# Normalising tokens from PSUM on VectorE instead of from SBUF on GpSimd, in a convolution-attention and mixture kernel on one Trainium2 core

## Chip, core and metric

The kernel runs on one core of one Trainium2 chip. A core has TensorE (matrix products, in the profile PE for the products and PEld for loading the stationary operand), VectorE (DVE), ScalarE (ACT), GpSimd (POOL) and SyncE (SP), which here only issues transfers. The engines run side by side, each takes its own instructions strictly in order, and they wait for each other through semaphores. SBUF is the working memory, PSUM the smaller memory into which TensorE writes. The metric is the device time of one execution in microseconds (us); a profile of one execution is the other source. All data is 32-bit floating point.

## What is computed

Eight images of 128 channels and 36 x 36 = 1296 positions pass through two layers. Cut to what matters here:

```python
# layer 0: group norm, then a convolution-attention block, added to x
q = conv3x3(x1); k = conv3x3(x1); v = conv3x3(x1)         # keys and values on 34 x 34 positions
a = einsum('ncd,nqd->ncq', v, softmax(einsum('ncd,ncq->nqd', k, q)))
x = x + conv1x1(tanh(conv1x1(concat([x1, a]))))
# layer 1: additive attention over the 1296 tokens of each image
t = tokens(x); y = layernorm(t)                           # over the 128 channels
s[i, j] = sum_d w[d] * tanh(q[i, d] + k[j, d]) + bw       # q, k: linear maps of y
t = t + softmax(s, axis=-1) @ y
# 64 experts, each picks 8 tokens of every image
z = layernorm(t)
gate = softmax(z @ gate_w.T, axis=tokens); top 8 per expert; gather; two layers; scatter-add
```

The tanh of every pair of tokens is the bulk of the work. The kernel writes it through products of exponentials: for each pair of token blocks it forms numerators n and denominators d by matrix products of features `qf` and `kf`, and needs n/d summed over the feature groups.

## The kernel before

**The main loop.** The pairwise stage is cut into units (image b, chunk c of 432 query tokens, tile j of 128 key tokens): 8 x 3 x 11 = 264 units. Ten of the eleven tiles have 12 slots each, the last tile (16 remaining tokens) has 3, so there are 2952 slots, in one static order. Each slot p issues, in this order: `take_turns(p)` (what background steps have to do outside TensorE); `numerators(p)`, two products into two PSUM buffers `n` (L793, or L800 for the short tile); `denominators(p + 3)`, two products into `d` and the logarithm of both by ScalarE (L815), and on every second slot one exponential over two slots' worth (L818), which makes 1/d; `terms(p)`, in which VectorE multiplies n by 1/d; and `matmul_turn(p)`, which lets background work put matrix products behind the slot's own. In 8 of 12 slots VectorE writes two products `rp` (L846) and GpSimd adds them to a running sum `accp` (L851 for the first, L853 after); in the other 4 VectorE multiplies in PSUM and adds to its own sum `accd` (L835 to L842). At the end of a unit GpSimd folds both sums (L860, L863) and ScalarE exponentiates (L878). `rp` has three buffers, so VectorE may run about two slots ahead of GpSimd and no more.

**Background work.** Everything else is written as generators in four lanes: `first_of_all` (query features), `urgent` (`attend`), `gates` (`gating`) and `background` (`normal`, `conv_keys`, `layer0`, `tokens` and `keys` of the next image). A generator yields either `step(rest)` (run my next part in take_turns, after `rest` slots) or `matmuls(rest)` (my next part issues matrix products), and `TAKE` after products, so that their reader runs one slot later. Products are counted in columns plus 20 each (`bmm` L237, `turned_to` L241 for transposes); a slot earns 370 of them, and while the balance is negative only `first_of_all` gets a turn. The order of the instructions on every engine comes out of this when the program is built; nothing is decided on the chip. For the first image all this runs ahead of the main loop, one generator after the other (`drain`).

**PSUM.** The pool `ps_n` has four buffers. The two `n` of every slot and the buffer of every background group (`aux`) come out of it in turn, so a background buffer that is read late holds up a later slot's products.

**The four places that the change touches.**

- `layer0`, per chunk of 432 positions: scores `s0`, exponentials `ex` on ScalarE (L381), their total on GpSimd (`total`, L374), ten products with the values in five pairs, each pair summed in a PSUM buffer `pa0` and added to `ax` in SBUF by VectorE (L395 the first, L397 the others, with a factor 1/D). Then the total over partitions by a product with ones (`pt0`), its reciprocal `ri` by two ScalarE instructions (L405, L406), a product `px1`, and VectorE's `ax * ri` (L412) and sum into `hp` (L413).
- `tokens`: the image is transposed into token rows, three PSUM buffers of four, four and three tiles (`tpl`), copied to `tok` in SBUF (L510, L516), sent to DRAM, and its mean and variance taken (L525, L526). After the reciprocal root on GpSimd (`rsqrt`, L218), GpSimd normalises the 11 tiles from `tok` into `xh` (L538), two at a time, one slot between. `xh` is transposed back into `xT` (`tpc`, L556).
- `attend`, four times per chunk: 11 products over the exponentials in two groups of six and five (`pa1`). VectorE copies the first group to `sums` (L625), adds the second (L628), takes the reciprocal of the last column (L630), and adds the scaled row to the token in `t2` (L631), then takes mean and variance (L635, L636).
- `gate_logits`: `t2` is transposed (`tp2`, L241), copied to `tt` (L676) and sent to DRAM; GpSimd normalises the 12 tiles of `t2` in place (L681), two at a time; then they are transposed again into `xc` (L691) and multiplied by the gating weights (L696). For the last image this runs per chunk, behind each `attend`.

**After the loop** come the last chunk's attending and gating, the experts with 32 MB of weights, and the scatter by matrix products.

Of the kernel before, what the change touches and what calls it, by code (L numbers as in the profile page):

```python
# [17 lines left out]
D = HV * WV  # L18
# [46 lines left out]
def kernel(  # L65
# [55 lines left out]
    with ExitStack() as loop, ExitStack() as score:  # L121
# [25 lines left out]
        def chunk_tile(name):  # L147
            return chunks.tile([128, CH], F32, tag="chunk", name=name)

        def aux(name):  # L150
            return ps_n.tile([128, 512], F32, tag="n", name=name)
# [177 lines left out]
        def layer0(b):  # L329

            r = xs[b][:, :N]
            k = convolved.pop("k")
            while gates:
                yield step()
            wv_t = load_taps(w_v, "wv_t")
            v = big_tile("v0")
            wq_t = load_taps(w_q, "wq_t")
            yield matmuls(3)
            for r0, nr in KROWS:
                yield from conv_turns(  # L340
                    wv_t, (r0, nr), 1, 1, WV, v[:, r0 * WV : (r0 + nr) * WV]
                )
            yield matmuls(1)

            vw = big_tile("vw")[:DT, : NDT * C].rearrange("p (j c) -> p j c", c=C)
            for g in range(0, NDT, 4):
                some = DTILES[g : g + 4]
                tp = aux("pvw")
                for j, (o, n) in enumerate(some):
                    bmm(tp[:n, j * C : (j + 1) * C], v[:, o : o + n], wh_s[:, 1, :],  # L350
                       start=True, stop=True)
                yield TAKE
                full = sum(n == DT for _, n in some)
                nc.vector.tensor_copy(
                    vw[:, g : g + full, :],
                    tp[:DT, : full * C].rearrange("p (j c) -> p j c", c=C),
                )
                for j in range(full, len(some)):
                    n = some[j][1]
                    nc.vector.tensor_copy(vw[:n, g + j, :], tp[:n, j * C : (j + 1) * C])  # L360
                yield matmuls()
            hp = big_tile("hpre")[:, :N]
            for c in range(NCH):
                cols = slice(c * CH, (c + 1) * CH)
                q = chunk_tile("q0")
                yield from conv_turns(wq_t, (c * RC, RC), 0, 0, W, q)
                yield matmuls(1)
                tot = chunk_tile("tot0")
                ex = []

                def total(j):
                    n = DTILES[j][1]
                    of = ex[0] if j == 1 else tot
                    nc.gpsimd.tensor_add(tot[:n], of[:n], ex[j][:n])  # L374

                for o, n in DTILES:
                    ps = aux("s0")
                    bmm(ps[:n, :CH], k[:, o : o + n], q, start=True, stop=True)
                    yield TAKE
                    e = chunk_tile("e0")  # L380
                    nc.scalar.activation(e[:n], ps[:n, :CH], AF.Exp)  # L381
                    ex.append(e)
                    if len(ex) > 2:
                        total(len(ex) - 2)
                    yield matmuls()
                ax = chunk_tile("ax0")
                for j0 in range(0, NDT, 2):
                    pa = aux("pa0")
                    for j in (j0, j0 + 1):
                        n = DTILES[j][1]  # L390
                        bmm(pa[:, :CH], vw[:n, j, :], ex[j][:n], start=(j == j0), stop=(j > j0))
                    yield TAKE
                    if j0 == 0:
                        total(NDT - 1)
                        nc.vector.tensor_scalar(ax, pa[:, :CH], 1.0 / D, None, ALU.mult)  # L395
                    else:
                        nc.vector.scalar_tensor_tensor(  # L397
                            ax, pa[:, :CH], 1.0 / D, ax, ALU.mult, ALU.add
                        )
                    yield matmuls()  # L400
                pt = aux("pt0")
                bmm(pt[:, :CH], ones[:DT], tot[:DT], start=True, stop=True)
                yield TAKE
                ri = chunk_tile("ri0")
                nc.scalar.activation(ri, pt[:, :CH], AF.Ln, scale=1.0 / D)  # L405
                nc.scalar.activation(ri, ri, AF.Exp, scale=-1.0)  # L406
                yield matmuls(1)
                px = aux("px1")
                bmm(px[:, :CH].rearrange("p (a b) -> p a b", b=W), wh_s[:, 0, :],
                   xpad[:, 1 + c * RC : 1 + (c + 1) * RC, 1 : 1 + W], start=True, stop=True)  # L410
                yield TAKE
                nc.vector.tensor_mul(ax, ax, ri)  # L412
                nc.vector.tensor_add(hp[:, cols], px[:, :CH], ax)  # L413
                yield matmuls()
            yield step(2)
            nc.scalar.activation(hp, hp, AF.Tanh, bias=hb)
            nc.scalar.preload_act_table_set(LNEXP)
            yield matmuls(2)
            for c in range(NCH):
                cols = slice(c * CH, (c + 1) * CH)  # L420
                po = aux("po0")
                bmm(po[:, :CH], wo_s, hp[:, cols], start=True, stop=True)
                yield TAKE
                nc.vector.scalar_tensor_tensor(
                    r[:, cols], po[:, :CH], bo_s, r[:, cols], ALU.add, ALU.add
                )
                yield matmuls()
# [63 lines left out]
        def tokens(b):  # L491
# [40 lines left out]
            rsqrt(rs, ve)  # L532
            xh = big_tile("xh")[:, : NKT * (C + 1)].rearrange("p (t c) -> p t c", c=C + 1)
            nc.gpsimd.memset(xh[:, :, C : C + 1], 1.0)
            yield step()
            for t in range(NKT):
                n = KT[t][1]
                nc.gpsimd.tensor_scalar(  # L538
                    xh[:n, t, :C], tok[:n, t, :], mv[:n, t, 0:1], rs[:n, t : t + 1],
                    ALU.subtract, ALU.mult,  # L540
                )
                if t % 2 == 1:
                    yield step()
            xT = big_tile("xT")[:, :N]
            yield matmuls(2)
            for g in range(0, NKT, 4):
# [54 lines left out]
        def attend(b, c, es):  # L601
# [8 lines left out]
            for i in range(TPC):  # L610
                at = c * TPC + i
                nc.sync.dma_start(t2[:T, at, :], tokd[b][at * T : (at + 1) * T])
                sums = two.tile([T, C + 1], F32, tag="sums", name="sums")
                for some in (range(6), range(6, NKT)):
                    pa = aux("pa1")[:T, : C + 1]
                    for j in some:
                        if j < NKT - 1:
                            e, v = es[j][:, i * T : (i + 1) * T], xh[:, j, :]
                        else:
                            rows = slice(32 * i, 32 * i + REM)  # L620
                            e, v = es[j][rows, :T], xr[rows]
                        bmm(pa, e, v, start=(j == some[0]), stop=(j == some[-1]))
                    yield TAKE
                    if j < NKT - 1:
                        nc.vector.tensor_copy(sums, pa)  # L625
                        yield matmuls()
                    else:
                        nc.vector.tensor_add(sums, pa, sums)  # L628
                inv = small.tile([T, 1], F32, tag="inv", name="inv")
                nc.vector.reciprocal(inv, sums[:, C : C + 1])  # L630
                nc.vector.scalar_tensor_tensor(  # L631
                    t2[:T, at, :], sums[:, :C], inv, t2[:T, at, :], ALU.mult, ALU.add
                )
                st = small.tile([T, 6], F32, tag="t2_st", name="t2_st")
                nc.vector.bn_stats(st, t2[:T, at, :])  # L635
                nc.vector.bn_aggr(mv[:, at, :], st)  # L636
                yield matmuls()
# [11 lines left out]
        def gate_logits(b, chunks):  # L649
# [23 lines left out]
            for c in chunks:  # L673
                tp, tt = turned(c, "t2T")
                yield TAKE
                nc.vector.tensor_copy(tt, tp[:, :CH])  # L676
                nc.sync.dma_start(t2d[b][:, c * CH : (c + 1) * CH], tt)
                yield matmuls()
            yield step()
            for j, t in enumerate(tiles):  # L680
                nc.gpsimd.tensor_scalar(  # L681
                    t2[:T, t, :], t2[:T, t, :], mv[:, t, 0:1], rs[:, j : j + 1],
                    ALU.subtract, ALU.mult,
                )
                if t % 2 == 1:
                    yield step()
            yield matmuls(2)
            for c in chunks:
                tp, xc = turned(c, "xc")
                yield TAKE  # L690
# [458 lines left out]
```

## Time and profile before

| | |
|---|---|
| median of three runs | 6428.76 us (6428.02 to 6435.07) |
| the profiled execution | 6428.41 us |
| its span, first to last instruction | 6426.7 us |
| PE busy | 6054.8 us (94%) |
| ACT busy | 5354.6 us (83%) |
| DVE busy | 4900.4 us (76%) |
| POOL busy | 4798.1 us (75%) |
| mean granted TensorE clock | 0.966 |

Busy time is the union of an engine's instructions; matrix products are pipelined, so a busy PE is not PE at its peak. Beside busy time the profile has groups of instructions (line, engine, names of what is written and read, shapes, count, busy time, mean duration of one in ns, idle time of the engine before them and what ended it), the waits (which engine's instruction was released by whose, in all), the chain (the work that ended last, followed back from the last instruction) and a timeline. A line of a group can be that of a helper: all background products stand under L237 and all background transposes under L241, told apart by the names of their tiles.

### The profile page before, as it was taken

The numbers are of one execution on the slowest core, as the hardware profiler recorded it, in microseconds if no ns is written. First come the engines' busy times: TensorE is split into PE (matmuls) and PEld (weight loads), VectorE is DVE, ScalarE is ACT, GpSimd is POOL, SyncE is SP. The second block draws the span as 40 slices with busy tenths as digits, with TensorE's granted clock in tenths as the row PEclk, the third lists the DMA queues.
The fourth block names the chain that finished last, engine by engine and source line by source line (L and its number), as shares of the span: only waits on it lengthen the run. The fifth ranks groups of instructions, "written<-read, shape, count | busy, mean of one in ns | idle before, by whom it ended". The sixth has DMA issues, their size and how long they took to land.

```text
span 6426.7 us, 106771 instructions
## 1 busy us (share of the span) xinstructions
PE 6054.8 (94%) x40448; PEld 2813.9 (44%) x40448; DVE 4900.4 (76%) x9315; ACT 5354.6 (83%) x5426; POOL 4798.1 (75%) x2966
## 2 busy tenths in 40 slices
PE   8999999999999999999999999999999999999986
PEld 4444444444444444444444444444444444544432
DVE  3687778877788777888788887887778877778862
ACT  1788898888888888888888888888888888989970
POOL 3677777787777877777787787778777787888870
PEclk9999999999999999999999999999999999999997
DMA  0200011000110002100111001100011000100017
GB/s 28 66 31 23 22 63 36 30 24 27 56 46 19 24 27 68 33 26 22 44 47 38 22 23 53 43 32 25 20 63 43 23 24 27 61 26 28 24 66 253
DMA packets 155284, 265.78 MB, mean 41 GB/s; under 512 B 53712, under 2 KB 79824, under 8 KB 154768
## 3 DMA queue, kind: packets, MB, share of 16 engines
q1 hardware_dynamic: 154768, 258.95, 12.5%
q8 instruction: 318, 5.21, 0.3%
q14 instruction: 198, 1.62, 0.1%
HBM read 196.81 MB, written 61.83 MB: 40 GB/s over the span
## 4 chain that ended last, share of the span: by engine, by line
PE 67%; DVE 12%; ACT 7%; issue 7%; POOL 6%; DMA 1%; SPq 0%; POOLq 0%; DVEq 0%; ACTq 0%
PE n L793 30%; PE d L793 10%; PE pc L237 7%; PE pa L237 6%; ACT lq L815 5%; DVE n L840 3%; DVE rp L846 3%; PE s L237 3%; PE pk L237 3%; PE pq L237 2%; DVE accd L842 2%; POOL accp L853 2%; DVE t L631 1%; PE n L800 1%; POOL t L681 1%
## 5 line engine op out<-in xcount | busy, mean ns | idle before, releaser
L853 POOL TENSOR_TENSOR accp<-accp,rp 128x864 f32<-128x864 f32 x1464 | 2965.2, 2025 | 1028.0 <-DVE rp L846 975.3
L793 PE MATMUL n<-qf,kf 32*128 32x432 f32 (+1 forms) x11520 | 3239.2, 579 | 93.4 <-DVE rp L846 47.0
L815 ACT ACTIVATE lq<-d 128x864 f32<-128x864 f32 x2952 | 2552.6, 882 | 690.7 <-PE d L793 643.3
L793 PE MATMUL d<-qf,kf 32*128 32x432 f32 (+1 forms) x11520 | 2876.6, 568 | 21.2 <-ACT lq L815 16.4
L846 DVE TENSOR_TENSOR rp<-n,lq 128x432 f32<-128x432 f32 x3984 | 2202.6, 600 | 623.7 <-PE d L793 399.3
L818 ACT ACTIVATE lq<-lq 128x1728 f32<-128x1728 f32 x1488 | 2429.0, 1632 | 47.1
L793 PEld LDWEIGHTS n<-qf,kf 32*128 32x128 f32 (+1 forms) x11520 | 1167.1, 187 | 1703.4 <-DVE rp L846 586.3
L793 PEld LDWEIGHTS d<-qf,kf 32*128 32x128 f32 (+1 forms) x11520 | 1038.8, 188 | 392.2 <-issue 254.1
L840 DVE TENSOR_TENSOR n<-n,lq 128x432 f32<-128x432 f32 x1440 | 811.7, 608 | 280.1 <-PE n L793 239.2
L842 DVE TENSOR_TENSOR accd<-n,accd 128x432 f32<-128x432 f32 x1440 | 867.4, 602 | 24.7
L851 POOL TENSOR_TENSOR accp<-rp 128x864 f32<-128x864 f32 x264 | 533.8, 2022 | 221.1 <-DVE rp L846 217.5
L237 PE MATMUL pa<-xh,e 128*108 128x129 f32 x1920 | 262.6, 284 | 55.6 <-DVE rp L846 34.7
L860 POOL TENSOR_TENSOR accp<-accp 128x432 f32<-128x432 f32 x264 | 290.8, 1101 | 16.2
L237 PEld LDWEIGHTS pa<-xh,e 128*108 128x108 f32 x1920 | 223.3, 175 | 179.1 <-DVE rp L846 107.4
L594 POOL TENSOR_SCALAR qf<-qf,cs_s 128x432 f32<-128x432 f32 x192 | 262.7, 1374 | 42.0 <-ACT qf L593 42.0
L863 POOL TENSOR_TENSOR accd<-accp,accd 128x432 f32<-128x432 f32 x240 | 265.6, 1107 | 28.5 <-DVE accd L842 10.4
L237 PE MATMUL s<-q,k 128*116 128x432 f32 x480 | 229.8, 570 | 3.3 <-DVE q L260 2.1
L237 PEld LDWEIGHTS pk<-xT,a_k 128*128 128x128 f32 x1408 | 172.2, 193 | 109.8 <-DVE accd L842 27.6
L374 POOL TENSOR_TENSOR tot<-tot,e 116x432 f32<-116x432 f32 x192 | 212.0, 1104 | 6.1
L835 DVE TENSOR_TENSOR accd<-n,lq 128x432 f32<-128x432 f32 x240 | 144.9, 604 | 91.6 <-PE n L793 60.5
L381 ACT ACTIVATE e<-s 116x432 f32<-116x432 f32 x240 | 125.0, 521 | 106.6 <-PE s L237 105.5
L237 PE MATMUL pk<-xT,a_k 128*128 128x128 f32 (+1 forms) x1408 | 203.2, 288 | 2.6 <-DVE accd L842 2.3
(175 smaller groups left out, 4144.4 us busy)
## 6 DMA issues: line engine op xcount, KB each, us to landing
kf<-kd SPq DMA_DIRECT2D x240, 512.0 KB
kd<-ks SPq DMA_DIRECT2D x160, 256.0 KB
w<-in_weight_dram SPq DMA_DIRECT2D x32, 1024.0 KB
x<-in_x_dram SPq DMA_DIRECT2D x8, 648.0 KB
t<-tokd SPq DMA_DIRECT2D x96, 54.0 KB
t2d<-t2T SPq DMA_DIRECT2D x24, 216.0 KB
res<-t2d SPq DMA_DIRECT2D x8, 648.0 KB
out_dram<-res SPq DMA_DIRECT2D x8, 648.0 KB
```

The costliest lines, as they stand in the source:

```text
L237: mm(out, lhsT, rhs, **kw)
L594: nc.gpsimd.tensor_scalar(qf[:, 1, :], qf[:, 0, :], cs_s[:, q : q + 1], None, ALU.mult)
L793: mm(outs[h][:, :CH], kf[rows[h], q, :], qf_of[b, c, q][rows[h], part, :], start=True, stop=True)
L815: nc.scalar.activation(lq[:, o : o + 2, :], d[:, :, :CH], AF.Ln)
L818: nc.scalar.activation(some, some, AF.Exp, scale=-1.0)
L840: mult(ns[h], ns[h], lq[:, o + h, :])
L842: nc.vector.tensor_add(live["d"], ns[h], live["d"])
L846: mult(rp[:, h, :], ns[h], lq[:, o + h, :])
L851: nc.gpsimd.tensor_add(live["p"], live["r"], rp)
L853: nc.gpsimd.tensor_add(live["p"], live["p"], rp)
L860: nc.gpsimd.tensor_add(s[:, 0, :], s[:, 0, :], s[:, 1, :])
L863: nc.gpsimd.tensor_add(d, s[:, 0, :], d)
```

## The change

In `tokens` and in `gate_logits` the normalisation is no longer made by GpSimd from SBUF. TensorE transposes the image (or the transposed tokens `tt`) once more into PSUM, and VectorE normalises from there into SBUF. In `attend` the second group's sum, its reciprocal and the scaled addition read PSUM. In `layer0` the total over partitions and its reciprocal come before the last pair of products, the factor 1/D is dropped (it cancelled), and the last partial sum is added in PSUM and multiplied by `ri` from there.

```diff
 layer0
                 ax = chunk_tile("ax0")
+                ri = chunk_tile("ri0")
                 for j0 in range(0, NDT, 2):
-                    pa = aux("pa0")
+                    if j0 == NDT - 2:
+                        pt = aux("pt0")
+                        bmm(pt[:, :CH], ones[:DT], tot[:DT], start=True, stop=True)
+                        yield TAKE
+                        nc.scalar.activation(ri, pt[:, :CH], AF.Ln)
+                        nc.scalar.activation(ri, ri, AF.Exp, scale=-1.0)
+                        yield matmuls()
+                    pa = aux("pa0")[:, :CH]
...
                     if j0 == 0:
                         total(NDT - 1)
-                        nc.vector.tensor_scalar(ax, pa[:, :CH], 1.0 / D, None, ALU.mult)
+                        nc.vector.tensor_copy(ax, pa)
+                    elif j0 < NDT - 2:
+                        nc.vector.tensor_add(ax, pa, ax)
                     else:
-                        nc.vector.scalar_tensor_tensor(
-                            ax, pa[:, :CH], 1.0 / D, ax, ALU.mult, ALU.add
-                        )
+                        nc.vector.tensor_add(pa, pa, ax)
+                        nc.vector.tensor_mul(ax, pa, ri)
                     yield matmuls()
-                pt = aux("pt0")
-                bmm(pt[:, :CH], ones[:DT], tot[:DT], start=True, stop=True)
-                yield TAKE
-                ri = chunk_tile("ri0")
-                nc.scalar.activation(ri, pt[:, :CH], AF.Ln, scale=1.0 / D)
-                nc.scalar.activation(ri, ri, AF.Exp, scale=-1.0)
-                yield matmuls(1)
                 px = aux("px1")
...
                 yield TAKE
-                nc.vector.tensor_mul(ax, ax, ri)
                 nc.vector.tensor_add(hp[:, cols], px[:, :CH], ax)
 tokens
-            yield step()
-            for t in range(NKT):
-                n = KT[t][1]
-                nc.gpsimd.tensor_scalar(
-                    xh[:n, t, :C], tok[:n, t, :], mv[:n, t, 0:1], rs[:n, t : t + 1],
-                    ALU.subtract, ALU.mult,
-                )
-                if t % 2 == 1:
-                    yield step()
+            yield matmuls()
+            for g in range(0, NKT, 4):
+                tp = aux("tpn")
+                some = list(range(g, min(g + 4, NKT)))
+                for t in some:
+                    o, n = KT[t]
+                    turned_to(tp[:n, (t - g) * C : (t - g + 1) * C], r[:, o : o + n], ident)
+                yield TAKE
+                for t in some:
+                    n = KT[t][1]
+                    nc.vector.tensor_scalar(
+                        xh[:n, t, :C], tp[:n, (t - g) * C : (t - g + 1) * C],
+                        mv[:n, t, 0:1], rs[:n, t : t + 1], ALU.subtract, ALU.mult,
+                    )
+                yield matmuls()
 attend
-                    else:
-                        nc.vector.tensor_add(sums, pa, sums)
+                nc.vector.tensor_add(pa, pa, sums)
                 inv = small.tile([T, 1], F32, tag="inv", name="inv")
-                nc.vector.reciprocal(inv, sums[:, C : C + 1])
+                nc.vector.reciprocal(inv, pa[:, C : C + 1])
                 nc.vector.scalar_tensor_tensor(
-                    t2[:T, at, :], sums[:, :C], inv, t2[:T, at, :], ALU.mult, ALU.add
+                    t2[:T, at, :], pa[:, :C], inv, t2[:T, at, :], ALU.mult, ALU.add
                 )
 gate_logits
-                yield matmuls()
-            yield step()
-            for j, t in enumerate(tiles):
-                nc.gpsimd.tensor_scalar(
-                    t2[:T, t, :], t2[:T, t, :], mv[:, t, 0:1], rs[:, j : j + 1],
-                    ALU.subtract, ALU.mult,
-                )
-                if t % 2 == 1:
-                    yield step()
-            yield matmuls(2)
+                yield matmuls(1)
+                tp = aux("tp3")
+                for j in range(TPC):
+                    turned_to(tp[:T, j * C : (j + 1) * C], tt[:, j * T : (j + 1) * T], ident)
+                yield TAKE
+                for j in range(TPC):
+                    t = c * TPC + j
+                    nc.vector.tensor_scalar(
+                        t2[:T, t, :], tp[:T, j * C : (j + 1) * C],
+                        mv[:, t, 0:1], rs[:, t - tiles[0] : t - tiles[0] + 1],
+                        ALU.subtract, ALU.mult,
+                    )
+                yield matmuls(1)
             for c in chunks:
                 tp, xc = turned(c, "xc")
```

More of the change, by code (lines that the diff above doesn't have):

```diff
@@ L386, in layer0 @@
                 ax = chunk_tile("ax0")
+                ri = chunk_tile("ri0")
                 for j0 in range(0, NDT, 2):
-                    pa = aux("pa0")
+                    if j0 == NDT - 2:
[6 more added lines that the diff above has]
+                    pa = aux("pa0")[:, :CH]
                     for j in (j0, j0 + 1):
                         n = DTILES[j][1]
-                        bmm(pa[:, :CH], vw[:n, j, :], ex[j][:n], start=(j == j0), stop=(j > j0))
+                        bmm(pa, vw[:n, j, :], ex[j][:n], start=(j == j0), stop=(j > j0))
                     yield TAKE
```

## The prediction

> **What bounds the kernel now.** I read the busy times first, then the chain, the waits, the groups by shape, the windows around the two normalisations, and the timeline inside them. From the page:
>
> ```profile
> PE 6054.8 (94%) x40448; PEld 2813.9 (44%) x40448; DVE 4900.4 (76%) x9315; ACT 5354.6 (83%) x5426; POOL 4798.1 (75%) x2966
> PE 67%; DVE 12%; ACT 7%; issue 7%; POOL 6%; DMA 1%; SPq 0%; POOLq 0%; DVEq 0%; ACTq 0%
> ```
>
> The second line is the chain: TensorE sets the pace in most places, GpSimd 6% and VectorE 12% of the span. Summed by name, the chain's pieces hold POOL t L681 57.5 us, POOL xh L538 32.2 and DVE t L631 83.8. These three are what the change attacks. The waits of VectorE on GpSimd, and who waits for L538:
>
> ```profile
> DVE rp L846 <- POOL accp L851: 78.1, 32, 8.7
> PEld tpc L241 <- POOL xh L538: 21.8, 17, 9.0
> ```
>
> The groups by shape (count | busy us, mean ns):
>
> ```profile
> L631 DVE SCALAR_TENSOR_TENSOR t<-sums,inv,t 108x128 f32<-108x128 f32 x96 | 87.9, 915 | 29.0 <-DMA t<-tokd 25.7
> L681 POOL TENSOR_SCALAR t<-t,t_mv,t_rs 108x128 f32<-108x128 f32 x96 | 75.0, 792 | 0.1
> L538 POOL TENSOR_SCALAR xh<-tok,ln_mv,ln_rs 128x128 f32<-128x128 f32 x80 | 62.5, 793 | 0.1
> L628 DVE TENSOR_TENSOR sums<-pa,sums 108x129 f32<-108x129 f32 x96 | 28.0, 292 | 18.2 <-PE pa L237 17.4
> L314 DVE TENSOR_SCALAR xpad<-px,bxn 128x432 f32<-128x432 f32 x24 | 15.9, 662 | 3.0 <-PE px L237 3.0
> L676 DVE COPY t2T<-tp 128x432 f32<-128x432 f32 x24 | 14.3, 597 | 0.0
> ```
>
> L631 reads two SBUF tensors and takes 915 ns; L628, as long a row, reads one from PSUM and takes 292. By line, L631 ranges from 350 to 1841 ns. The timeline of one token normalisation (start, us; idle before in brackets):
>
> ```profile
> 3927.53 2.01 POOL L851 TENSOR_TENSOR accp<-rp 128x864 f32<-128x864 f32 x1
> ...
> 3929.57 1.12 DVE L846 TENSOR_TENSOR rp<-n,lq 128x432 f32<-128x432 f32 x2 [4.40 <-POOL accp L851]
> ...
> 3930.23 1.60 PE L793 MATMUL n<-qf,kf 32*128 32x432 f32 x2 [2.84 <-DVE rp L846]
> ...
> 3932.65 0.89 ACT L815 ACTIVATE lq<-d 128x864 f32<-128x864 f32 x1 [3.07 <-PE d L793]
> ```
>
> Four L538 fill GpSimd from 3924.44 to 3927.53, its sum L851 is late, all three `rp` are taken, VectorE stands 4.40 us, then TensorE 2.84 and ScalarE 3.07. Reading VectorE's idle stretches one by one, such stalls behind L538 add to about 34 us and behind L681 to about 32 (up to 8.75 each). The windows of two such places (PE, PEld, DVE, ACT, POOL busy, clock):
>
> ```profile
> 3316.00:3336.00 20.00, 15.78 (x76) 6.89 (x74) 15.82 (x27) 13.70 (x13) 19.85 (x19) 0.83 0.04 7
> 3911.00:3936.00 25.00, 20.17 (x88) 9.29 (x88) 17.09 (x33) 17.35 (x18) 21.54 (x21) 0.73 0.07 22
> ```
>
> GpSimd is full in the first, the others are not, and the clock is down. Elsewhere, with no background at all, a 12-slot unit takes 19.9 us (starts of L815 in the last image), close to ScalarE's twelve L815 and six L818; with background it takes 22 to 27.
>
> **What the Trainium skill says.** "SBUF — State Buffer", Who interferes with whom: a VectorE instruction with two SBUF inputs and a GpSimd instruction that reads SBUF exclude each other, the later one waits in full; with at most one SBUF input outside the two-port modes there is no contention. The trace agrees: L631 350 to 1841 ns, L628 282 to 296. "VectorE: DVE Perf Modes", Why PSUM operands drop a tier: a PSUM source excludes the two-port modes; L676 and L314, from PSUM, show no spread. "PSUM — Partial Sum Buffer", The four PSUM rules: GpSimd can't read PSUM, so the normalisation has to change engine. "TensorE: Matmul & The Clock Gate", What's actually happening: the clock halves after an idle window; 0.73 and 0.83 above against 0.98 over a whole image agree.
>
> **The change part by part**, against the span of 6426.7 us.
>
> *GpSimd relieved.* 184 instructions of 0.79 us (88 + 96) go: 145 us, 18 per image. GpSimd keeps the roots (L218, 2.1 to 2.3 us) and its sums. The stalls of 34 + 32 us end. Not all of that was lost: in the case shown ScalarE, the floor of an empty slot, lost 3.07 of 4.40, 70%. I take 75%: -50. The half-speed stretches behind them (one to two of 6.8 us at each place) cost products drawn out to double length; most of that overlaps, -6.
>
> *L631.* The source becomes PSUM, one SBUF input is left, so 350 ns: 96 x (915 - 352) = 54 us of VectorE. In the case at 3523.18 (1.84 us) TensorE then stood 1.16 us for the next products, 0.78 of the excess; short excesses hide. I take 0.6: -32. The add and the reciprocal keep their durations (292, 164); the PSUM buffer is held for reciprocal and addition too, 0.5 us, but VectorE does both before the slot's own products anyway: 0.
>
> *Transposes added.* 23 per image, 184 in all. Four L241 took 0.59 us in the timeline (3306.13), so 0.15 each: 27 us of TensorE.
>
> *VectorE added.* 184 scalings from PSUM. There is no such row; L676 to L314 shows a pointer scalar at +65 ns, and L631 without contention (one pointer) is 350. So 0.35, bounded by 0.29 (L628) and 0.42 (a second pointer at +65), and consecutive instructions overlap 0.08 (two L846 in 1.12): 1.2 us for a group of four. They stand in VectorE's queue ahead of a slot's products, whose PSUM buffers TensorE waits for.
>
> *Groups on the path.* In the loop there are 21 token groups (images 1 to 7) and 23 gating groups (images 0 to 6, and two chunks of the last): 44. Each costs between 0 (VectorE had 3 to 8 us free in the windows above, TensorE 4 to 5) and 0.59 + 1.2 = 1.8, in series. In those windows three groups ask 3.6 us of VectorE, so much hides, but in units with attending VectorE is full. I take 0.8: +35. That the token path now waits on three more turns is paid by the five single-slot rests and GpSimd's 8.5 us that go.
>
> *Layer 0.* L412 (816 ns, of two SBUF inputs) becomes one from PSUM at 605: 24 x 0.21 = 5 us off; other instructions are exchanged one for one. `ri` is now wanted one slot after ScalarE gets it: the last pair ends about 2 us after `pt0`, and in one case `ri` was ready 3.2 us after `pt0` ended. Waits up to 1 us on 24, up to +24; I take +5, in all 0.
>
> *Before the loop.* L538 x11 takes 8.54 us on the chain with nothing beside it. Three groups pipelined, first transposes 0.6 and eleven scalings 3.3: -4.5. *After the loop*: L681 x4 3.12 us against transposes 0.6 and scalings 1.2: -1.5 (weights load meanwhile; the chain waits here on gating).
>
> No transfer is added or moved past another; `tt` and the image are held longer, `tok` shorter. Sum: -50 - 6 - 32 + 35 + 0 - 4.5 - 1.5 = -59. Span 6367.7; the execution adds 1.7 (6428.41 - 6426.7): 6369.4, and the median before is 0.35 above that execution. I say **6369**.
>
> **Rivals.**
> *VectorE takes GpSimd's place.* Its queue is in order and the group stands ahead of products, so groups cost 1.6 each: 44 x 0.8 = 35 more, 6404. For: units with attending have VectorE busy 22.8 of 24 us (3522 to 3546). Against: the normalising windows have room.
> *All of it comes off.* Stalls -66, L631 at 0.8 (-43), clock -10, groups at 0.4 (+18), ends -6: -107, 6321. For: the chain holds 57.5 + 32.2 + about 50 us of it.
> *Slower: PSUM buffers held.* One ring of four serves products and background. Fully exposed, 44 groups in series cost 79 us, the buffer of each of 96 attends half a microsecond more (48), of 24 last partial sums 0.6 (14): 141, against 94 gained: 6475. It decides once more than 94 us are exposed. For: TensorE's loads wait 586.3 us on rp L846 already. Against: VectorE's order makes most of it no wait.
> *No effect.* Stalls replaced by equal ones of TensorE, since it is at 94%: 6428. Against: the windows show TensorE idle there.
>
> **How the numbers follow.** The case of the sum (6345 to 6390) 0.50; VectorE in place 0.23; all off 0.09; slower 0.12; no effect 0.06. About 0.2%, 13 us, is what a measurement of this kernel tells from no change. Faster 0.50 + 0.23 + 0.09 = 0.82, same 0.06, slower 0.12. From 6322 to 6413 takes in the first two with their unknown costs and the edge of the third: 0.8.
>
> **What would show it.** L631 near 350 ns without spread. POOL busy near 4650. VectorE's wait on L851 from 78 to under 20 us. The new scalings 0.35 us each, and VectorE's busy time about unchanged (+50 of them, -54 of L631, -5 of L412). TensorE's clock above 0.966. The second rival would show VectorE's queue full, and TensorE's waits on it grown, in the slots with `tpn` and `tp3`. Wrong would be: scalings over 0.6 us, long waits for `ri` ahead of the multiplication by it, or units that keep their 28 to 29 us at the normalisations.

## The result and the profile after

| | before | after |
|---|---|---|
| median (range) of 4 runs | 6428.39 us (6424.59 to 6435.07) | 6335.55 us (6322.62 to 6347.35) |
| profiled execution | 6428.41 us | 6322.62 us |
| its span | 6426.7 us | 6320.9 us |
| mean granted TensorE clock | 0.966 | 0.974 |
| TensorE at half speed, all stretches together | 438 us | 328 us |

The ratio is 0.9854, with a 95% interval of 0.9833 to 0.9875: 93 us faster. The forecast was 6369, a gain of 59. The time lies in its range, below the case of the sum (6345 to 6390). The profiled execution is the fastest of the four, 13 us below the median; what follows is read from it.

Lines have moved: L793 is now L802, L815 L824, L818 L827, L842 L851, L846 L855, L851 L860, L853 L862, L631 L637. New are L546 (scaling of the tokens into `xh`), L691 (scaling in the gating) and L634 (the second sum in `pa`). The busy times and the shares of the chain, from the page of the kernel after:

```profile
PE 6067.5 (96%) x40632; PEld 2825.9 (45%) x40632; DVE 4894.6 (77%) x9499; ACT 5360.3 (85%) x5426; POOL 4655.2 (74%) x2782
PE 68%; DVE 11%; ACT 8%; issue 7%; POOL 4%; DMA 1%; SPq 1%; POOLq 0%; DVEq 0%; ACTq 0%
```

184 instructions have left GpSimd (2966 to 2782, 143 us of busy time) and 184 have come to VectorE, whose busy time did not grow (4900.4 to 4894.6). GpSimd's share of the chain went from 6% to 4%. The groups by shape show why VectorE's sum is even (count | busy us, mean ns | idle before, and what ended it):

```profile
L637 DVE SCALAR_TENSOR_TENSOR t<-pa,inv,t 108x128 f32<-108x128 f32 x96 | 33.7, 351 | 28.8 <-DMA t<-tokd 25.3 <-DVE inv L636 0.3
L691 DVE TENSOR_SCALAR t<-tp,t_mv,t_rs 108x128 f32<-108x128 f32 x96 | 32.6, 403 | 1.3 <-PE tp L241 1.3
L241 PE MATMUL tp<-ident,t2T 128*108 128x128 f32 x96 | 18.6, 326 | 1.3 <-DVE t2T L682 0.8
L634 DVE TENSOR_TENSOR pa<-pa,sums 108x129 f32<-108x129 f32 x96 | 28.7, 299 | 9.0 <-PE pa L237 7.3
L546 DVE TENSOR_SCALAR xh<-tpn,ln_mv,ln_rs 128x128 f32<-128x128 f32 x80 | 27.4, 404 | 11.3 <-POOL ln_rs L218 8.8 <-PE tpn L241 2.5
L241 PE MATMUL tpn<-ident,x 128*128 128x128 f32 x80 | 14.7, 305 | 2.8 <-DVE accd L851 2.8
```

L637 takes 351 ns where L631 took 915: 54 us less busy time. The scalings take 403 ns each and add 63 (3.1 for the short tiles). Transposes take 35 us of TensorE (14.7 + 18.6, and 2.2 for the short tiles), not 27. TensorE's busy time as a whole grew by 12.7 us only, so its other products took some 23 us less (a difference of busy times, so an estimate), with 110 us less at half speed. Its idle time, the span less its busy time, fell from 371.9 to 253.4 us.

The waits (engine, line, what it waited for: us in all, times, longest):

```profile
ACT lq L824 <- PE d L802: 515.1, 675, 4.6
PEld n L802 <- DVE rp L855: 505.7, 888, 1.4
PEld n L802 <- DVE xh L546: 12.2, 14, 1.6
DVE rp L855 <- POOL accp L860: 8.2, 6, 1.9
PEld n L802 <- DVE t L691: 6.6, 12, 0.8
```

and the first two of them in the kernel before:

```profile
ACT lq L815 <- PE d L793: 643.3, 719, 9.1
PEld n L793 <- DVE rp L846: 586.3, 926, 8.6
```

VectorE's wait for GpSimd's first sum is 8.2 us where it was 78.1. Two other waits are shorter too: TensorE's loads for `n` wait 81 us less on `rp` and never longer than 1.4 us at a time, and ScalarE waits 128 us less for the denominators. New are 12.2 + 6.6 = 18.8 us in which TensorE's loads wait for the scalings. Summed by name, the chain holds 17.4 us of `t` L637 (83.8 of L631 before), none of the GpSimd scalings (57.5 + 32.2 before), and 17.9 + 17.1 = 35.0 us of the new ones.

From the starts of L815 and L824: the loop begins at 182.1 us (188.2 before), image 0 takes 753.2 us (762.7), images 1 to 6 take 751 to 758 (764 to 768), and from the last slot's start to the end there are 192.6 us (193.9). The unit (chunk 2, tile 6) of images 2 to 6, where tokens were normalised, takes 22.2 to 23.0 us instead of 29.3 to 29.5. Not every unit gained: (2,4) went from 27.5 to between 29.3 and 30.6.

### The profile page after: what moved, and what is told of

The parts are those of the page before. It is cut to its first block, busy times and chain, and to the rows that moved or that the text cites. A ratio compares the mean times of both kernels' runs of the same rounds, so it can differ in the third digit from the quotient of the medians.

```text
span 6320.9 us, 107144 instructions
## 1 busy us (share of the span) xinstructions
PE 6067.5 (96%) x40632; PEld 2825.9 (45%) x40632; DVE 4894.6 (77%) x9499; ACT 5360.3 (85%) x5426; POOL 4655.2 (74%) x2782
## 3 DMA queue, kind: packets, MB, share of 16 engines
q1 hardware_dynamic: 154768, 258.95, 12.8%
## 4 chain that ended last, share of the span: by engine, by line
PE 68%; DVE 11%; ACT 8%; issue 7%; POOL 4%; DMA 1%; SPq 1%; POOLq 0%; DVEq 0%; ACTq 0%
PE n L802 31%; PE d L802 10%; PE pc L237 8%; PE pa L237 7%; ACT lq L824 5%; DVE n L849 3%; PE s L237 3%; DVE rp L855 3%; PE pk L237 2%; POOL accp L862 2%; DVE accd L851 2%; PE pq L237 1%; PE n L809 1%; PE d L809 1%; POOL qf L601 1%
## 5 line engine op out<-in xcount | busy, mean ns | idle before, releaser
L862 POOL TENSOR_TENSOR accp<-accp,rp 128x864 f32<-128x864 f32 x1464 | 2965.3, 2026 | 1137.6 <-DVE rp L855 1045.7
L802 PE MATMUL n<-qf,kf 32*128 32x432 f32 (+1 forms) x11520 | 3244.9, 575 | 54.4 <-DVE accd L851 10.0
L824 ACT ACTIVATE lq<-d 128x864 f32<-128x864 f32 x2952 | 2559.8, 883 | 587.2 <-PE d L802 515.1
L802 PE MATMUL d<-qf,kf 32*128 32x432 f32 (+1 forms) x11520 | 2889.0, 564 | 41.4 <-ACT lq L824 37.9
L855 DVE TENSOR_TENSOR rp<-n,lq 128x432 f32<-128x432 f32 x3984 | 2201.6, 600 | 565.5 <-PE d L802 374.4
L827 ACT ACTIVATE lq<-lq 128x1728 f32<-128x1728 f32 x1488 | 2431.1, 1634 | 47.1
L802 PEld LDWEIGHTS n<-qf,kf 32*128 32x128 f32 (+1 forms) x11520 | 1173.4, 185 | 1659.2 <-DVE rp L855 505.7
L802 PEld LDWEIGHTS d<-qf,kf 32*128 32x128 f32 (+1 forms) x11520 | 1036.0, 187 | 405.0 <-issue 236.0
L851 DVE TENSOR_TENSOR accd<-n,accd 128x432 f32<-128x432 f32 x1440 | 867.9, 603 | 24.7
L860 POOL TENSOR_TENSOR accp<-rp 128x864 f32<-128x864 f32 x264 | 534.7, 2026 | 145.1 <-DVE rp L855 143.6
L869 POOL TENSOR_TENSOR accp<-accp 128x432 f32<-128x432 f32 x264 | 291.8, 1105 | 17.1
L237 PEld LDWEIGHTS pk<-xT,a_k 128*128 128x128 f32 x1408 | 171.9, 193 | 108.6 <-issue 27.5
L237 PE MATMUL pa<-e,vw 116*128 116x432 f32 x480 | 206.2, 556 | 3.9 <-DVE accd L851 3.0
```

What stands on the lines that cost most here:

```text
L237: mm(out, lhsT, rhs, **kw)
L802: mm(outs[h][:, :CH], kf[rows[h], q, :], qf_of[b, c, q][rows[h], part, :], start=True, stop=True)
L824: nc.scalar.activation(lq[:, o : o + 2, :], d[:, :, :CH], AF.Ln)
L827: nc.scalar.activation(some, some, AF.Exp, scale=-1.0)
L851: nc.vector.tensor_add(live["d"], ns[h], live["d"])
L855: mult(rp[:, h, :], ns[h], lq[:, o + h, :])
```

## The experiments

Each ratio is to the kernel before, run on the same chip in the same sitting. Differences to the kernel after, which wasn't run again beside them, are taken between such ratios; with the intervals given, they are uncertain by about 16 us.

**One part at a time.** Four kernels, each the kernel before with one part of the diff: `tokens` alone, `gate_logits` alone, `attend` alone, `layer0` alone. The edit of each is the hunk of that name in the diff above; the last one is:

```diff
 layer0, the kernel before
+                    if j0 == NDT - 2:
+                        pt = aux("pt0")
...
+                        nc.scalar.activation(ri, pt[:, :CH], AF.Ln)
...
-                pt = aux("pt0")
...
-                nc.vector.tensor_mul(ax, ax, ri)
```

> The kernel before with the change of tokens alone. Theory of the sum: stalls behind L538 of 34 us at 75% (-25.5), half of the clock's share (-3), 21 groups at 0.8 us (+17), -4.5 before the loop: -16 us. Theory that all comes off (stalls in full, groups at 0.4): -35 us. VectorE in GpSimd's place (groups at 1.6): about 0. If the parts do not act for themselves but by the new order of the turns, the four parts alone need not sum to the -93 us of the whole.

> The kernel before with the change of gate_logits alone. Theory of the sum: stalls behind L681 of 32 us at 75% (-24), clock -3, 23 groups at 0.8 us (+18.4), -1.5 after the loop: -10 us. All comes off: -29 us. VectorE in GpSimd's place: +8 us.

> The kernel before with the change of attend alone: the scaled addition at 350 ns instead of 915, 54 us of VectorE. Theory of the sum: 0.6 of it, -32 us. All comes off: -43 us or more. If TensorE or ScalarE follow at once in the attending units: under -15 us.

> The kernel before with the change of layer0 alone. Theory of the sum: 0 us (5 us of VectorE off, 5 us of waiting for ri on). If waiting for ri counts: up to +24 us. If the port of L412 counts in full: -5 us or some more.

| part alone | median us | ratio (95%) | us | VectorE's long stops behind GpSimd's scalings |
|---|---|---|---|---|
| none (before) | | | | 34 (`xh`) + 32 (`t`) |
| tokens | 6398.02 | 0.9949 (0.9937 to 0.9962) | -33 | 47 (`t`) |
| gates | 6460.53 | 1.0053 (1.0039 to 1.0067) | +34 | 51 (`xh`) |
| attend | 6384.75 | 0.9931 (0.9917 to 0.9945) | -44 | 35 + 33 |
| layer 0 | 6503.42 | 1.0112 (1.0098 to 1.0126) | +72 | 50 + 47 |

The parts sum to +29 us, the whole is -93: they don't add. The last column shows one reason. It is summed, to within 3 us, from VectorE's idle stretches of over 0.6 us ahead of an `rp` that ended with GpSimd's sum, where one of GpSimd's scalings ran just before that sum. Each of these parts except `attend` changes how many turns the background takes, and so shifts the scalings that are still on GpSimd against the slots; there the stops were longer: the tokens' stops grew from 34 to 51 us when the gating's were taken away, the gating's from 32 to 47 when the tokens' were, and both together from 66 to 97 when only layer 0 changed. VectorE's wait on the first GpSimd sum of a unit, with layer 0 alone (78.1 before):

```profile
DVE rp L847 <- POOL accp L852: 99.2, 22, 6.9
```

So taking one kind of scaling away makes the stops behind the other kind longer; with both kinds gone there are none left.

The stops don't explain these times alone. With the gating alone they are 15 us shorter than before, and the kernel is 34 us slower. There, unit (2,10), the short tile, takes 11.6 to 12.8 us in images 1 to 6 instead of 6.4 to 8.6, some 30 us in all, and for 7.5 to 10.3 us of it TensorE is at half speed (3.4 to 6.2 before); why the stretches of half speed fall there isn't settled. With layer 0 alone TensorE's idle time is that of before (376.4 us, before 371.9), while the same 40448 products keep it busy 80 us longer, with 582 us at half speed instead of 438: in that run the loss lies in slower products and not in longer waits.

**The parts taken out of, or put back into, the whole**, with the order of everything else held. First the kernel after with attending as it was:

```diff
 attend, the kernel after
-                nc.vector.tensor_add(pa, pa, sums)
+                    else:
+                        nc.vector.tensor_add(sums, pa, sums)
-                nc.vector.reciprocal(inv, pa[:, C : C + 1])
+                nc.vector.reciprocal(inv, sums[:, C : C + 1])
...
-                    t2[:T, at, :], pa[:, :C], inv, t2[:T, at, :], ALU.mult, ALU.add
+                    t2[:T, at, :], sums[:, :C], inv, t2[:T, at, :], ALU.mult, ALU.add
```

> The changed kernel with attend as before (sums, reciprocal and scaled addition from SBUF); every engine keeps the changed kernel's order of instructions. If the scaled addition's wait for GpSimd is worth what it was alone: some 30 to 45 us over the changed kernel, 0.990 to 0.9925 of the kernel before. If another engine follows at once now: under 15 us.

6393.74 us, ratio 0.9943 (0.9929 to 0.9957): 57 us over the kernel after. Its group of scaled additions:

```profile
L638 DVE SCALAR_TENSOR_TENSOR t<-sums,inv,t 108x128 f32<-108x128 f32 x96 | 92.5, 964 | 26.9 <-DMA t<-tokd 23.6
```

96 x (964 - 351) = 59 us of VectorE's time, and the kernel loses 57: as measured nothing of it hides, and with the uncertainty of 16 us at least two thirds of it count.

Second, the kernel after with GpSimd's load put back. GpSimd makes 184 scalings of the same shapes again, into a spare tile that nobody reads, so little but GpSimd's time is added (its values in the gating are not those wanted).

```diff
 tokens, the kernel after (gate_logits likewise)
                 for t in some:
                     n = KT[t][1]
+                    nc.gpsimd.tensor_scalar(
+                        spare[:n, t % 2, :], tok[:n, t, :], mv[:n, t, 0:1], rs[:n, t : t + 1],
+                        ALU.subtract, ALU.mult,
+                    )
                     nc.vector.tensor_scalar(
...
```

> The changed kernel, and GpSimd scales the 184 tiles as well, from SBUF into a spare tile that nobody reads, at the turn at which VectorE does (the result is not changed). All other engines keep their order. If GpSimd's lateness was the loss: +50 to +66 us over the changed kernel, 0.993 to 0.996. If the gain comes from elsewhere: under 10 us.

6388.12 us, ratio 0.9933 (0.9920 to 0.9945): 51 us over the kernel after. The wait that had gone is back in part:

```profile
DVE rp L864 <- POOL accp L869: 35.0, 20, 4.7
```

Nobody waits for the spare tile, and VectorE's own busy time grew by 8 us only, so most of the 51 us comes from work that GpSimd does late, its sums among it, and from what that sets back. In the profiled execution TensorE stands 24 us longer than in the kernel after, and its products, the same in number, take 37 us longer, with 389 us at half speed instead of 328: a good part of a late sum's cost shows as slower products.

Third, the kernel after with every new scaling issued twice (the second writes the same values over the first):

```diff
 the kernel after
-                for t in some:
+                for t in some + some:
...
-                for j in range(TPC):
+                for j in (*range(TPC), *range(TPC)):
```

> The changed kernel, with each of the 184 scalings on VectorE issued twice (the same result is written again), about 60 us of VectorE more, all else in the same order. If a group costs 0.4 to 0.8 us on the path, the second half of it: +15 to +35 us. If VectorE has become the bound at these places: +60 us or more. If all is covered: under 8 us.

6402.61 us, ratio 0.9954 (0.9941 to 0.9966): 64 us over the kernel after, for 184 x 0.32 = 59 us of VectorE (consecutive ones start 0.32 us apart). TensorE's loads behind them:

```profile
PEld n L802 <- DVE t L691: 43.9, 39, 2.1
PEld n L802 <- DVE xh L546: 38.5, 30, 2.9
```

With one set they waited 18.8 us, with two 82.4. The difference is 64 us, as large as the loss, but that the two are equal is in part chance: TensorE's idle time grew by 34 us, and its products took 39 us longer, with 418 us at half speed instead of 328. In the chain the scalings grow from 35.0 to 88.0 us. So a second set hides hardly at all, while loads wait little behind the first.

**VectorE without the transposes.** The kernel before, with the two GpSimd instructions given to VectorE as they stand, from SBUF. No transposes, no new buffers, the order of before.

```diff
 the kernel before, L538 and L681
-                nc.gpsimd.tensor_scalar(
+                nc.vector.tensor_scalar(
```

> The kernel before, with the scalings issued on VectorE instead of GpSimd, in place from SBUF, two at a time: no transposes, all in the order of before. If only GpSimd's relief counts: -40 to -60 us. If SBUF operands make VectorE wait for GpSimd as in L631, about 0.5 us each: no gain, -15 to +30 us, and the scalings last 0.3 to 2 us each.

6445.3 us, ratio 1.0026 (1.0017 to 1.0035): 17 us slower than before. Its groups:

```profile
L681 DVE TENSOR_SCALAR t<-t,t_mv,t_rs 108x128 f32<-108x128 f32 x96 | 80.3, 879 | 0.6 <-POOL t_rs L218 0.6
L538 DVE TENSOR_SCALAR xh<-tok,ln_mv,ln_rs 128x128 f32<-128x128 f32 x80 | 59.0, 782 | 21.7 <-POOL ln_rs L218 21.7
```

and the same instruction by its shortest, median and longest time, here from SBUF:

```profile
L681 DVE TENSOR_SCALAR t<-t,t_mv,t_rs x96: 330/340/2171, 1014.0 to 6292.2; 108x128 f32<-108x128 f32 x96
```

and in the kernel after from PSUM:

```profile
L691 DVE TENSOR_SCALAR t<-tp,t_mv,t_rs x96: 399/402/411, 993.4 to 6174.0; 108x128 f32<-108x128 f32 x96
```

From SBUF the median is shorter, but 26 of the 96 take over 2 us, about as long as one of GpSimd's sums. The Trainium skill, "SBUF — State Buffer", Who interferes with whom, names `tensor_scalar` among the instructions that can enter a two-port mode and then exclude GpSimd. The spread fits that, though the trace doesn't show the mode itself; from PSUM there is next to no spread (399 to 411). Relief of GpSimd alone is thus worth nothing if VectorE pays for it from SBUF: 139 us of VectorE come for 137 off GpSimd. The transposes, 35 us of TensorE, are what makes the exchange pay.

**Is it the order of the turns?** The gain of the whole could have been a lucky order. Layer 0 in the changed order, but summing and multiplying in SBUF, so that no PSUM buffer waits for the reciprocal:

```diff
 layer0 of the kernel with layer 0 alone
-                        nc.vector.tensor_add(pa, pa, ax)
-                        nc.vector.tensor_mul(ax, pa, ri)
+                        nc.vector.tensor_add(ax, pa, ax)
+                        nc.vector.tensor_mul(ax, ax, ri)
```

> The kernel before with layer 0's steps in the changed order (total over partitions and reciprocal ahead of the last pair of products), but the last partial sum goes to SBUF and is multiplied by the reciprocal from there, so that no PSUM buffer is held for it. Layer 0 alone, done as in the change, cost 71 us (1.0112). If the shifted order of turns is its cause: +55 to +75 us here too, 1.009 to 1.012, unit (2,10) at 11 to 12 us again. If it is the PSUM buffer held while VectorE waits for the reciprocal: 0 to +20 us, 1.000 to 1.003. Between the two, both have a part.

6509.43 us, ratio 1.0130 (1.0114 to 1.0145): +84. The buffer isn't it: where the sum is made makes no difference that can be told (1.0112 with it in PSUM). What is left is the order in which the steps come. The stops behind GpSimd's scalings are at most 32 us longer (49 + 49 against 66), as above. TensorE's idle time is 20 us longer, and its products, the same in number, take 50 us longer, with 505 us at half speed instead of 438. As expected, unit (2,10) is long again: 11.1 to 12.4 us in images 1 to 6, for 7.8 to 11.1 of them at half speed. That is some 25 us; the rest is spread over other units by up to 2.3 us each and isn't settled.

Then both kernels with another pace, which moves all turns and adds nothing:

```diff
-PACE = 370
+PACE = 380
```

> The kernel before with the columns that a slot earns for background products set to 380 instead of 370; no instruction is added or taken away, only the turns at which background steps come move. If the order of turns is worth tens of us in itself, this moves the time by 15 to 60 us in one direction or the other (ratio outside 0.998 to 1.002). If it isn't, within 0.2%.

> The changed kernel with 380 columns a slot instead of 370. If the gain of the change is that of its instructions (GpSimd relieved, attending from PSUM, less the new scalings), it stays 60 to 125 us under the kernel before with 380, whatever that does. If the gain is mostly a luckier order of turns, it shrinks under 40 us or turns its sign.

Before: 6442.59 us, ratio 1.0018 (1.0010 to 1.0026). After: 6326.69 us, ratio 0.9842 (0.9828 to 0.9855). So this shift of the order is worth +12 us in one kernel and nothing that can be told (-8) in the other; the pair is 113 us apart, where it was 93. In both orders that were tried the gain is there, so it isn't that of one lucky order.

**Half of the scalings on ScalarE.** Since VectorE is exposed at these places, every second scaling went to ScalarE, as an identity with scale and bias from the same PSUM buffer; GpSimd makes the bias with two small instructions.

```diff
 gate_logits, the kernel after (tokens likewise)
+            nc.gpsimd.tensor_tensor(nm, mv[:, tiles[0] : tiles[-1] + 1, 0], rs, ALU.mult)
+            nc.gpsimd.tensor_scalar(nm, nm, -1.0, None, ALU.mult)
...
+                    if j % 2:
+                        nc.scalar.activation(
+                            t2[:T, t, :], tp[:T, j * C : (j + 1) * C], AF.Identity,
...
+                        )
+                        continue
```

> The changed kernel with every second of the 184 scalings made by ScalarE from PSUM (identity with scale and bias), and two small GpSimd instructions per group of roots for the bias; the order of everything else is held. A second set of scalings on VectorE cost 64 us, so VectorE is exposed there: half of them off it should give 20 to 30 us against the changed kernel, 0.981 to 0.983 of the kernel before. If ScalarE, which has the longest work of a slot after TensorE, is exposed as well, 92 instructions of about 0.3 us on it take 15 to 30 us back: no difference to the changed kernel, or 10 to 20 us more.

6374.52 us, ratio 0.9914 (0.9900 to 0.9928): 39 us slower than the kernel after. Neither expectation had this size. ScalarE took 450 to 457 ns for a scaling where 300 had been reckoned with, and there is a second cost. The timeline of one group (start, us, idle before in brackets):

```profile
4053.48 1.64 ACT L846 ACTIVATE lq<-lq 128x1728 f32<-128x1728 f32 x1
4053.81 0.40 DVE L710 TENSOR_SCALAR t<-tp,t_mv,t_rs 108x128 f32<-108x128 f32 x1
...
4055.03 0.44 ACT L704 ACTIVATE t<-tp,t_nm,t_rs 108x128 f32<-108x128 f32 x1
4055.51 0.41 DVE L710 TENSOR_SCALAR t<-tp,t_mv,t_rs 108x128 f32<-108x128 f32 x1 [1.29 <-ACT t L704]
...
4055.95 0.46 ACT L704 ACTIVATE t<-tp,t_nm,t_rs 108x128 f32<-108x128 f32 x1 [0.48 <-DVE t L710]
...
4056.46 0.86 PE L821 MATMUL n<-qf,kf 32*128 32x432 f32 x2 [1.70 <-ACT t L704]
```

The two engines don't share the group, they hand it to and fro: ScalarE comes to its first piece only after its exponential of 1.64 us, VectorE waits for that, ScalarE for VectorE, and TensorE for the last. From the first scaling's start to the last one's end there are 2.6 us; on VectorE alone four take 1.36. TensorE's idle time is only 11 us longer than in the kernel after; its products take 47 us longer, with 434 us at half speed instead of 328. All pieces go into one tile, and each waits for the one before it in the program; that the shared tile is the reason was not tried (two pieces in a row per engine, or two tiles, would tell).

## Why the prediction was right or wrong

**GpSimd relieved (-50, and -6 for the clock): right in the sum.** The load put back costs 51 us. The wait on the sum fell under the 20 us that I had named. The split isn't borne out: with the load put back TensorE's idle time grew by 24 us and the stretches of half speed by 61, half of which, 30 us, is an estimate of what slower products cost. By this estimate the clock's part was set too low and that of the stops too high, and that the sum came out is in part luck. It holds only for the whole: one half alone lets the other stall more.

**L631 (-32): the term that was mis-sized.** The duration was right, 351 ns without spread. The share of 0.6 that I took of its 54 us was not: put back in the changed kernel, 59 us of VectorE cost 57; taken out of the kernel before, 54 us give 44. As measured, the share is 0.8 to 1 (with the intervals, 0.65 and more); both values are above the 32 us of the forecast. I had drawn it from one case in which TensorE stood for 0.78 of the excess, and then lowered it for short excesses. But in the chain before, L631 alone held 83.8 us, almost all of its busy time of 87.9: VectorE was the last to arrive there. That view was at hand and spoke for a share near 1. By these readings it is 25 us of the 34 by which the time fell short of 6369; the groups give 13 more, and GpSimd's relief takes 5 back.

**Groups on the path (+35): perhaps too dear.** The cost of a scaling was 0.40 us (forecast 0.35, bounds 0.29 to 0.42), 0.32 from start to start, and a group of four 1.36 instead of 1.2. What of it is exposed can be read from TensorE's loads: 18.8 us. Another way: from -93, without -51 for GpSimd, -57 for L631 and -7 for the two ends, there remain +22 for scalings, transposes, layer 0 and the new order together. Both are below 35, by 13 us in the second reading, but that remainder carries the uncertainty of all the others, some 25 us, so that the term was too dear isn't shown. That a second set hides hardly at all is shown.

**Layer 0 (0): right as a count of instructions, and not the whole cost.** L408, the multiplication by `ri`, waited for ScalarE nowhere. But I priced a changed list of turns at nothing beyond its own instructions. Layer 0's shift of turns alone costs 72 to 84 us in the kernel before. In the whole this doesn't appear. Up to 32 us of it were stops behind scalings that are gone there; much of the rest shows as slower products, with more time at half speed, and why the whole is spared it is open.

**The ends (-4.5 and -1.5): the first right, the second not told.** The loop begins 6.1 us earlier. The end behind the last slot is 1.3 us shorter, but in the profiles of the other kernels, one execution each, it ranges from 191.6 to 197.3 us.

**The signs.** GpSimd's busy time (4655.2, forecast near 4650), VectorE's (-6, forecast -9) and the clock (0.974, above 0.966) came as named. The units at the old normalisation fell to 23 us, but (2,5) keeps 28.5 and (2,4) rose to between 29.3 and 30.6. The transposes took 0.18 to 0.19 us each on average, not 0.15.

**The rivals.** "All of it comes off" (6321) is the nearest to the profiled execution, 6322.62, and not for its reasons: it took 76 us for stalls and clock where 51 were measured, and 43 for L631 where 57 were. "VectorE takes GpSimd's place" put the groups at 70 us; they are at 22, though the doubled scalings show that it would be true of a little more work. Buffers held in PSUM, the slower case, don't show: TensorE's loads for `n` waited 15.0 us for the sum and 16.9 for the reciprocal of `attend` before, and now wait 4.4, 16.2 and 11.4 us (L637), 32 in all both times; and layer 0 costs the same with its sum in SBUF. "No effect" is out.

## What to carry to other kernels

The chain is a pointer to what hides, and not a price: L631, whose chain time of 83.8 us was nearly its busy time of 87.9, hid little or nothing, while GpSimd's scalings stood in the chain with 89.7 us, and their load put back cost 51. A relief of an engine that is late at certain turns can't be split into parts that add, because here each part that changed the turns moved the others against the loop; measure parts by taking them out of the finished whole with the order held. When work moves to VectorE beside a busy GpSimd, what it reads decides: from PSUM an instruction kept its time to 3%, from SBUF it ran from 330 to 2171 ns.

## What the runs showed of the hardware that was not expected

A VectorE instruction on one column can take longer than GpSimd's sum of 2.02 us. In the kernel before (shortest, median, longest):

```profile
L291 DVE SCALAR_TENSOR_TENSOR dev<-dev,gn_mv x8: 219/1952/3697, 20.3 to 4854.9; 128x1 f32<-128x1 f32 x8
```

The median hides the shape: four of the eight take 219 or 220 ns, the other four 3.69 to 3.70 us. At one of the long ones GpSimd goes from scalings into a sum without a stop:

```profile
2552.70 3.13 POOL L681 TENSOR_SCALAR t<-t,t_mv,t_rs 108x128 f32<-108x128 f32 x4
...
2554.13 3.69 DVE L291 SCALAR_TENSOR_TENSOR dev<-dev,gn_mv 128x1 f32<-128x1 f32 x1
...
2555.79 2.02 POOL L853 TENSOR_TENSOR accp<-accp,rp 128x864 f32<-128x864 f32 x1
```

L291 ends when the sum does, at 2557.8: it was not let in between the scalings, nor between the last of them and the sum. So its size of one column said nothing about its time.

Two units of the same program and the same place in an image can differ by 4 us. Unit (1,5) of the kernel after takes about 27 us in four of images 1 to 6 and 31 in the other two. In those two alone, a stretch of 6.83 us at half clock falls into it (at 3564.6 and 5073.3 us). The first begins like this:

```profile
3562.51 0.60 PE L809 MATMUL n<-qf,kf 32*32 32x108 f32 x32
...
3564.15 0.66 PE L809 MATMUL n<-qf,kf 32*32 32x108 f32 x32 [1.05 <-issue]
...
3566.48 3.25 PE L237 MATMUL pa<-e,vw 116*128 116x432 f32 x4
```

TensorE stands for 1.05 us for nothing that the profile names, between two halves of the short tile's products; the stretch at half clock begins 0.4 us after it resumes, and then four products take 3.25 us. In image 6 the stop is 0.65 us; at the same place in the other four images it is 0.31 us at most, and no stretch follows. So the units part at the stop. Stops of this kind have something in common: in the 14 profiles of this case there are 60 of over 0.4 us between 200 and 6000 us, and each ends 1.2 to 1.6 us after a packet of the queue that the page calls `instruction` (319 packets in the kernel after) has landed. In image 4 that packet lands 0.06 us after the unit's start and in image 6 0.4 us before it, in the other four 0.5 to 1.1 before. It looks as if TensorE waits there for its next instructions; nothing was changed to try it, nor whether the spread of the kernel after (25 us over four runs) comes from such stops.

ScalarE was no faster at scaling from PSUM than VectorE: 450 ns mean for 108 partitions and 457 for 128, beside 403 and 404.
